# Four graph layers in one pipeline: the transposed features made a stage earlier, and two steps added to the order of the work

## The chip, the cores and the metric

The kernel runs on one core of a Trainium2 chip. The metric is the device time of one launch in microseconds (us); the time of a kernel is the median of several runs. Before the change it is 5589.18 us (three runs, 5588.3 to 5589.55). In what follows PE is the tensor engine (matmuls; its weight loads are a row of their own, PEld), DVE the vector engine, ACT the scalar engine, POOL the general-purpose engine, and SP the engine that issues the DMAs.

## What is computed

Input x holds 64 graphs ("images") of 256 nodes with 128 features, adj their 256 x 256 adjacency matrices of zeros and ones, each row with a few tens of ones. Four layers follow each other, and each ends with a residual and a layernorm:

```python
def _layernorm(x, axis=-1, eps=1e-5):
    m = jnp.mean(x, axis=axis, keepdims=True)
    v = jnp.var(x, axis=axis, keepdims=True)
    return (x - m) / jnp.sqrt(v + eps)
# layer 0: maximum over the neighbours
p = x @ (W1 - W2); q = x @ W2
h = relu(p[:, :, None, :] + q[:, None, :, :] + b) * adj[..., None]
x = _layernorm(x + max(h, axis=2))
# layer 1: in, out and node representations (elu), two aggregations with adj, tanh of a product
# layer 2: two steps of normalised aggregation with elu between
# layer 3: for every pair of nodes a message
pre = m_j[:, None, :, :] + m_i[:, :, None, :] + b1
msg = gelu(layernorm(pre, g1, be1))
agg = einsum('bijo,bij->bio', msg, adj)
x = _layernorm(x + layernorm(concat([x, agg]) @ W2 + b2))
```

Layers 0 and 3 touch every edge: the maximum of layer 0, and in layer 3 a layernorm over the features and a Gelu for every edge. They are most of the work.

## The kernel before

**Edges as slots.** For each image the neighbours of every node are numbered, and the nodes are ordered by how many they have. Slot s of a node is its s-th neighbour, and 40 slots suffice. The slots, cut to the nodes that can have as many, make one line of 4800 columns for each half h of the neighbours (WIDTH, from RECTS, L27). A matrix `hot` of zeros and ones (in an 8-bit format) picks the neighbour of each column, so that one matmul with `hot` as the moving operand gathers features: L668 gathers q for layer 0 (three bf16 parts of q, so three matmuls per 512 columns), L731 gathers c for layer 3. L684 adds corrections for slots that a node lacks.

**Layer 0** (`layer_0`, L643): the features xn are transposed by PE (`to_features`, L201: two transposes L205 and a copy by ACT L207) into xT, multiplied with the weights w0qp (L650), and the neighbours' part is split in three (`split3`, L494: q by ACT, the rest by DVE L498 to L500). For each half and each 512 columns L668 and L684 fill a PSUM tile `bigp`; the first is copied by ACT into `lanes` (L686), DVE folds the others into it by maximum (`fold`, L481, recorded under L492 and L488). After the last one `total_m` (L691) is the maximum of the two lanes; PE transposes it (L694), ACT copies it to `mk` (L695), and L702 puts the nodes back into their own order.

**Layer 3** works on tiles of 1024 columns, 704 at the end: five tiles in each half, ten in all (TODO, L716). `sums_of` (L721) makes one tile of `pre`: L731 gathers, DVE adds the node's own part (L735), ACT squares (L739), PE sums the squares over the features (L746), ACT adds eps (`row`, L748), and a DMA lays the row into DRAM (`line`, L753). After every second tile the two rows are fetched as a small tile `vr` of up to 128 x 16 (L765), with a mask `fu` (L767); ACT takes the square root and DVE the reciprocal (`inverse_root`, L70 to L73), DVE multiplies by the mask (L772), and a DMA writes the scales to DRAM (`scale_line`, L774). In `last` (L828) a scale row is fetched, spread over all partitions (`rs_s`, L835), two tiles ahead of its use; DVE multiplies (L846), ACT takes the Gelu (L848), DVE folds by addition (`sums`, L492), and PE multiplies the fold by the weights (L867) and puts the nodes in order (L877). `sums_of` runs four tiles ahead (AHEAD). `inverse_root` also serves the layernorms (rs, L174) and the degrees (dinv, L270).

**Tables of ACT.** Sqrt, Exp, Tanh and Gelu need different function tables on ACT; wherever one follows another in ACT's order, the compiler puts a table load ahead of it.

**Stages and order.** An image passes four stages: `first` (slots and `hot`, L502), `second` (layers 0 and 1), `third` (layer 2 and the first four tiles of layer 3), `last` (the rest). In one step the four stages work on four successive images, 64 + 3 steps in all, written out without a loop (UNROLL, L40). The stages are Python generators; each `yield` ends a piece. `together` (L339) always takes the next piece of the generator that is least far along, measured as pieces taken over a weight; the weights are the numbers in STAGES (L886), which are the numbers of pieces. So another `yield` or another weight moves all pieces of a step against each other. What comes out is the order in which the pieces are recorded; a scheduler of the language then makes each engine's own list out of it, which need not follow the recorded order exactly. Each engine works its list strictly in order, and so does SP with its DMAs. PSUM is split into four tiles `mm` and four tiles `bigp`; a tile is reused when it has been read.

Of the kernel before, what the change touches and what calls it, by code (L numbers as in the profile page):

```python
# [9 lines left out]
F32 = mybir.dt.float32  # L10
BF16 = mybir.dt.bfloat16
AF = mybir.ActivationFunctionType
# [7 lines left out]
P = 128  # L20
# [23 lines left out]
def kernel(  # L44
# [9 lines left out]
    nc = tc.nc  # L54
# [15 lines left out]
    def inverse_root(t):  # L70

        nc.scalar.activation(t, t, AF.Sqrt)  # L72
        nc.vector.reciprocal(t, t)  # L73

    def load(src, shape, name):
        t = consts.tile(shape, F32, name=name)
        nc.sync.dma_start(t, src)
        return t
# [4 lines left out]
    def spread(src, name):  # L83
        return load(bass.AP(tensor=src.tensor, offset=src.offset, ap=[[0, P], [1, P]]), [P, P], name)

    w0 = load(l0_w.rearrange("(c p) o -> p c o", p=P), [P, 2, P], "w0")
    w0qp = consts.tile([P, 2, P], F32, name="w0qp")
    nc.vector.tensor_copy(w0qp[:, 0], w0[:, 1])
    nc.vector.tensor_sub(w0qp[:, 1], w0[:, 0], w0[:, 1])
    b0 = column(l0_b, "b0")  # L90
    b0s = spread(l0_b, "b0s")

# [27 lines left out]
    with tc.tile_pool(name="prep", bufs=1) as prep, tc.tile_pool(  # L120
        name="ps_prep", bufs=2, space=bass.MemoryType.PSUM
    ) as ps_prep:

        def transposed(dst, src, shape, name, part=lambda t: t):
            t = prep.tile(shape, F32, name=name)
            nc.sync.dma_start(t, src)
            for d, s in part(t) if dst is None else [(dst, t)]:
                pt = ps_prep.tile([P, P], F32, name="pt")
                nc.tensor.transpose(pt, s, ident)
                nc.vector.tensor_copy(d, pt)  # L130

        transposed(w1_ioT[:, :P], l1_w_in, [P, P], "w1_in")
        transposed(w1_ioT[:, P:], l1_w_out, [P, P], "w1_out")
        transposed(w1_nodeT, l1_w_node, [P, P], "w1_node")
        transposed(
            None, l1_w_upd.rearrange("o (c k) -> o c k", k=P), [P, 3, P], "w1_upd",
            lambda t: [(w1_updT[:, c], t[:, c]) for c in range(3)],
        )
        w3 = prep.tile([P, 2, P], F32, name="w3")
        nc.sync.dma_start(w3, l3_w1.rearrange("(c p) o -> p c o", p=P))  # L140
        w3m = prep.tile([P, 2], F32, name="w3m")
        nc.vector.tensor_reduce(w3m, w3, AX.X, ALU.add)
        nc.vector.tensor_scalar(w3m, w3m, 1.0 / P, None, ALU.mult)
        for c in range(2):
            nc.vector.tensor_scalar(w3c[:, c], w3[:, c], w3m[:, c:c + 1], None, ALU.subtract)
        b3 = prep.tile([P, 1], F32, name="b3")
        nc.sync.dma_start(b3, bass.AP(tensor=l3_b1.tensor, offset=l3_b1.offset, ap=[[1, P], [1, 1]]))
        invp = prep.tile([P, P], F32, name="invp")
        nc.vector.memset(invp, 1.0 / P)
        pb = ps_prep.tile([P, P], F32, name="pt")  # L150
        nc.tensor.matmul(pb[:, :1], invp, b3, start=True, stop=True)
        nc.vector.tensor_sub(b3c, b3, pb[:, :1])


    class Shared:
# [5 lines left out]
        def psum(self):  # L161
            return self.ps_mm.tile([P, 512], F32, name="mm")
# [173 lines left out]
    def by_half(pt):  # L336
        return pt[:, :N].rearrange("p (h d) -> p h d", h=H)
# [14 lines left out]
    def sparse(ctx):  # L352
# [102 lines left out]
        sh = Shared(work, state, ps_mm)  # L455
# [46 lines left out]
        def first(g, s):  # L502

            xn = state.tile([P, H, P], F32, name="x0", bufs=3)
# [25 lines left out]
            for hi in range(H):  # L530
                for h in range(H):
                    c = (hi * H + h) * 2
# [38 lines left out]
            permT = hold.tile([P, H, H, N], F32, name="permT")  # L571
# [17 lines left out]
            lack = hold.tile([ROWS, H, N], BF16, name="lack")  # L589
# [5 lines left out]
            for h in range(H):  # L595
                for hk in range(H):
                    c = (h * H + hk) * 2
# [10 lines left out]
            lack_t = state.tile([ROWS, H, g_n, g_w], BF16, name="lack_t")  # L608
# [15 lines left out]
            hot = hold.tile([P, H, WIDTH], FP8, name="hot")  # L624
# [8 lines left out]
            for h in range(H):  # L633
# [5 lines left out]
                    saturate=False,  # L639
                )  # L640
            s["hot"] = hot

        def layer_0(s):  # L643

            xn, hot, lack, lack_t, permT = (s[n] for n in ("xn", "hot", "lack", "lack_t", "permT"))
            xT = sh.to_features(xn, "xT_0", 1)
            yield
            pq = psum()
            for h in range(H):
                nc.tensor.matmul(  # L650
                    pq[:, h * N:(h + 1) * N], xT[:, h * P:(h + 1) * P], w0qp.rearrange("p c o -> p (c o)"),
                    start=True, stop=True,
                )
            pq = pq.rearrange("p (h c o) -> p h c o", h=H, c=2)
            q3 = work.tile([P, 3, H, P], BF16, name="q3")
            split3(q3, pq[:, :, 0])
            own = work.tile([P, H, P], F32, name="own")
            for h in range(H):
                nc.vector.tensor_add(own[:, h], pq[:, h, 1], b0s)
            yield  # L660
            mk = work.tile([P, H, H, P], F32, name="mk")
            for h in range(H):
                lanes = work.tile([P, 2, N], F32, name="lanes")
                for t0 in range(0, WIDTH, 512):
                    tl = min(512, WIDTH - t0)
                    pt = ps_big.tile([P, 512], F32, name="bigp")
                    for i in range(3):
                        nc.tensor.matmul(  # L668
                            pt[:, :tl], q3[:, i, h], hot[:, h, t0:t0 + tl], start=i == 0, stop=False
                        )  # L670
                    todo = []
                    for s0, n, w, at in pieces(t0, t0 + tl):
                        if s0 >= g_s0:
                            todo.append((pt[:, at:at + n * w], low, lack_t[:, h].rearrange("p s k -> p (s k)")))
                            continue
                        for i in range(n):
                            m = SURE[s0 + i]
                            if m < w:
                                c = at + i * w
                                todo.append((pt[:, c + m:c + w], pick_of(s0 + i), lack[:, h, m:w]))  # L680
                    if not todo:
                        todo.append((pt[:, :2], pick_of(0), lack[:, h, 0:2]))
                    for i, (o_, l_, r_) in enumerate(todo):
                        nc.tensor.matmul(o_, l_, r_, start=False, stop=i == len(todo) - 1)  # L684
                    if t0 == 0:
                        nc.scalar.copy(lanes, pt.rearrange("p (s k) -> p s k", s=2))  # L686
                    else:
                        fold(lanes, pt, t0, tl, ALU.max)
                    yield
                mx = work.tile([P, N], F32, name="total_m")  # L690
                nc.vector.tensor_max(mx, lanes[:, 0], lanes[:, 1])  # L691
                pt = psum()
                for hk in range(H):
                    nc.tensor.transpose(pt[:, hk * P:(hk + 1) * P], mx[:, hk * P:(hk + 1) * P], ident)  # L694
                nc.scalar.copy(mk[:, h], by_half(pt))  # L695
                yield
            pm = psum()
            for h in range(H):
                for hi in range(H):
                    c = h * N + hi * P  # L700
                    for hk in range(H):
                        nc.tensor.matmul(  # L702
                            pm[:, c:c + P], permT[:, h, hk, hi * P:(hi + 1) * P], mk[:, h, hk],
                            start=hk == 0, stop=hk == H - 1,
                        )
            yield
            m0 = work.tile([P, H, P], F32, name="m0")
            nc.scalar.copy(m0, by_half(pm))
            nc.vector.tensor_max(m0, pm[:, N:].rearrange("p (h d) -> p h d", h=H), m0)
            nc.vector.tensor_add(m0, m0, own)  # L710
            y = work.tile([P, H, P], F32, name="y", bufs=2)
            nc.vector.scalar_tensor_tensor(y, m0, 0.0, xn, ALU.max, ALU.add)
            s["x1"] = sh.node_tile("x1")
            yield from sh.layernorm(s["x1"], y)
# [6 lines left out]
        def sums_of(s, i):  # L721

            h, t0, tl = TODO[i]
            hot, c3, dT = s["hot"], s["c3"], s["dT"]
# [36 lines left out]
            n = at + tl  # L761
            rows = n // PIECE
            first_at = TODO[i - GROUP + 1][0] * WIDTH + TODO[i - GROUP + 1][1]
            vr = big.tile([P, PIECE], F32, name="vr")
# [3 lines left out]
                fu[:rows],  # L768
                s["fulls"].rearrange("h w -> (h w)")[first_at:first_at + n].rearrange("(p k) -> p k", k=PIECE),
            )  # L770
            inverse_root(vr[:rows])
            nc.vector.tensor_mul(vr[:rows], vr[:rows], fu[:rows])  # L772
            out_line = dram.tile([1, GROUP * TILE], F32, name="scale_line")
            nc.sync.dma_start(out_line[:, :n].rearrange("o (p k) -> (o p) k", k=PIECE), vr[:rows])  # L774
# [108 lines left out]


        U = next(u for u in (UNROLL, 8, 4, 2, 1) if B % u == 0)
        STAGES = [(last, 34), (third, 34), (second, 42), (first, 17)]  # L886

        def steps(g0):
            ss = [{} for _ in range(U)]
# [216 lines left out]
    with tc.tile_pool(name="flag", bufs=1) as fp, tc.tile_pool(  # L1106
        name="ps_flag", bufs=1, space=bass.MemoryType.PSUM
# [44 lines left out]
```

## Time and profile before

| | |
|---|---|
| median of three runs | 5589.18 us (5588.3 to 5589.55) |
| profiled execution, its own time | 5585.87 us |
| its span, first to last instruction | 5583.8 us |
| mean granted clock of PE | 0.876 |
| DMA moved | 365.17 MB, 65 GB/s |
| ACT table loads | 447 at L72, 447 at L848, 133 at L192, 63 at L252, 61 at L196, 1283 ns each |
| one step in the steady part | 85.0 us |

The profile is one execution, recorded by the hardware. Its page gives busy time by engine; the view of waits gives who waited for whom, in total; the view of groups gives each kind of instruction with its mean duration; the timeline shows instructions one after the other, with the idle time ahead of them in brackets and what ended it; the view by windows gives busy time and granted clock in stretches of time. "L735" is line 735 of the kernel as printed above. The engines run at the same time, and a wait costs something only if the engine that waits is late for the end.

### The profile page before, as it was taken

To read this page: it belongs to the slowest core of one execution; us is meant where nothing else is said; L and a number is where in the kernel's file an instruction comes from. 1 tells how busy PE (TensorE), PEld (TensorE's weight loads), DVE (VectorE), ACT (ScalarE), POOL (GpSimd) and SP (SyncE) were. 2 spreads that over 40 slices of the span, in tenths; PEclk is the share of its full clock that TensorE was granted. 3 is DMA by queue.
4 is the path that set the end of the run, shared out by engine and by line. 5 is a ranking of instruction groups with operands and counts; after the bars stand their busy time and mean duration, and the time that the engine had idled before them with its cause. 6 is when DMAs were issued, how large, how long until landed. Compare 5 with 4: busy or idle time off the path is not lost.

```text
span 5583.8 us, 83622 instructions
## 1 busy us (share of the span) xinstructions
PE 4511.0 (81%) x27408; PEld 2487.9 (45%) x27408; DVE 4805.5 (86%) x14654; ACT 4218.5 (76%) x6465; POOL 2.0 (0%) x10
## 2 busy tenths in 40 slices
PE   5888888888788888887887888888888878888884
PEld 3444444444444444444444444444444444444442
DVE  7788888898888888888988888889888888888886
ACT  2777777777777777777777777777777777777776
POOL 0000000000000000000000000000000000000000
PEclk8888888888888888888888888888888888888886
DMA  0212222222222122222222222221222222212212
GB/s 24 65 59 72 67 63 66 72 65 66 66 65 70 60 72 67 63 66 74 63 66 67 70 66 61 69 67 63 71 70 63 66 67 70 66 59 71 64 59 76
DMA packets 292814, 365.17 MB, mean 65 GB/s; under 512 B 151952, under 2 KB 210448, under 8 KB 292368
## 3 DMA queue, kind: packets, MB, share of 16 engines
q1 hardware_dynamic: 292368, 359.73, 20.8%
q8 instruction: 218, 3.57, 0.3%
q14 instruction: 228, 1.87, 0.1%
HBM read 345.07 MB, written 14.53 MB: 64 GB/s over the span
## 4 chain that ended last, share of the span: by engine, by line
PE 42%; DVE 34%; ACT 17%; issue 5%; DMA 3%; SPq 0%; DVEq 0%; POOL 0%; ACTq 0%; POOLq 0%
PE bigp L731 8%; PE bigp L668 8%; DVE lanes L492 8%; DVE pre L735 6%; ACT L72 6%; DVE hot L628 5%; DVE sums L492 5%; PE mm L867 4%; DVE pre L846 3%; PE mm L746 3%; PE mm L877 2%; PE mm L817 2%; PE mm L294 2%; DMA rs_s<-scale_line 2%; ACT sums L848 2%
## 5 line engine op out<-in xcount | busy, mean ns | idle before, releaser
L668 PE MATMUL bigp<-hot,q 128*128 128x512 fp8e4 (+1 forms) x3840 | 1117.5, 391 | 206.2 <-DVE lanes L492 179.7
L731 PE MATMUL bigp<-hot,c 128*128 128x512 fp8e4 (+1 forms) x3840 | 1010.6, 395 | 136.0 <-DVE pre L735 77.1
L735 DVE TENSOR_TENSOR pre<-bigp,dT 128x512 f32<-128x512 f32 (+6 forms) x1664 | 841.4, 534 | 252.2 <-PE bigp L731 245.9
L739 ACT ACTIVATE sq<-pre 128x1024 f32<-128x1024 f32 (+1 forms) x640 | 636.6, 995 | 273.2 <-DVE rs L73 196.9
L492 DVE TENSOR_TENSOR lanes<-bigp,lanes 128x512 f32<-128x512 f32 (+6 forms) x1536 | 769.3, 501 | 12.2 <-ACT vr L72 2.9
L846 DVE TENSOR_TENSOR pre<-pre,rs_s 128x1024 f32<-128x1024 f32 (+1 forms) x640 | 734.4, 1148 | 35.6 <-DMA rs_s<-scale_line 34.5
L492 DVE TENSOR_TENSOR sums<-pre,sums 128x1024 f32<-128x1024 f32 (+6 forms) x1024 | 628.3, 614 | 11.6 <-ACT pre L848 11.2
L848 ACT ACTIVATE pre<-pre,be,g 128x1024 f32<-128x1024 f32 (+1 forms) x512 | 600.0, 1172 | 11.0 <-DVE pre L846 6.9
L731 PEld LDWEIGHTS <-c 128*128 128x128 bf16 x3840 | 346.2, 102 | 544.5 <-issue 268.1
L848 ACT ACT_TABLE_LOAD x447 | 573.5, 1283 | 7.9
L72 ACT ACT_TABLE_LOAD x447 | 573.5, 1283 | 7.9
L748 ACT ACTIVATE row<-mm,eps_t 128x256 f32<-128x256 f32 (+1 forms) x640 | 293.5, 459 | 361.9 <-PE mm L746 351.0
L668 PEld LDWEIGHTS <-q 128*128 128x128 bf16 x3840 | 309.6, 100 | 514.9 <-DVE lanes L492 186.5
L746 PE MATMUL mm<-sq,ones 128*32 128x256 f32 (+1 forms) x5120 | 436.5, 418 | 113.7 <-ACT sq L739 110.7
L628 DVE TENSOR_SCALAR hot<-rank 128x512 fp8e4<-128x512 bf16 (+5 forms) x1536 | 485.4, 345 | 0.0
L684 PEld LDWEIGHTS <-pick 42*128 42x128 bf16 x2944 | 154.5, 95 | 449.6 <-issue 435.2
L650 PE MATMUL mm<-w0qp,xT 128*128 128x256 f32 x256 | 130.0, 662 | 266.3 <-ACT xT L207 266.3
L867 PE MATMUL mm<-w3u,sums 128*128 128x128 f32 x2048 | 293.8, 287 | 44.9 <-DVE sums L492 44.9
L867 PEld LDWEIGHTS mm<-w3u,sums 128*128 128x128 f32 x2048 | 258.7, 195 | 75.9 <-PE bigp L731 39.6
L684 PE MATMUL bigp<-lack,pick 42*128 42x36 bf16 (+16 forms) x2944 | 275.8, 187 | 0.0
L746 PEld LDWEIGHTS mm<-sq,ones 128*32 128x32 f32 x5120 | 107.2, 115 | 352.5 <-ACT sq L739 162.0
L73 DVE RECIPROCAL vr<-vr 128x16 f32<-128x16 f32 (+1 forms) x320 | 79.5, 249 | 161.7 <-ACT vr L72 161.6
(227 smaller groups left out, 7319.0 us busy)
## 6 DMA issues: line engine op xcount, KB each, us to landing
rs_s<-scale_line SPq DMA_DIRECT2D x512, 512.0 KB
rs_s<-scale_line SPq DMA_DIRECT2D x128, 352.0 KB
an<-in_adj SPq DMA_DIRECT2D x64, 256.0 KB
x<-in_x SPq DMA_DIRECT2D x64, 128.0 KB
line<-row SPq DMA_DIRECT2D x512, 4.0 KB
out<-o SPq DMA_DIRECT2D x64, 128.0 KB
fu<-fulls SPq DMA_DIRECT2D x192, 4.0 KB
vr<-line SPq DMA_DIRECT2D x192, 8.0 KB
```

The lines of the kernel that those rows point to most:

```text
L72: nc.scalar.activation(t, t, AF.Sqrt)
L492: nc.vector.tensor_tensor(lanes[:, :k, :w], src[:, i:i + k], lanes[:, :k, :w], op)
L628: nc.vector.tensor_scalar(hot[:, :, at:at + w], rank[:, :, :w], s0 + i + 1.0 - FAR, None, ALU.is_equal, saturate=False)
L668: nc.tensor.matmul(pt[:, :tl], q3[:, i, h], hot[:, h, t0:t0 + tl], start=i == 0, stop=False)
L684: nc.tensor.matmul(o_, l_, r_, start=False, stop=i == len(todo) - 1)
L731: nc.tensor.matmul(pt[:, :bl], c3[:, k, h], hot[:, h, t0 + b:t0 + b + bl], start=k == 0, stop=k == 2)
L735: nc.vector.tensor_add(block(pre[:, b:], n, w, at), block(pt, n, w, at), widen(dT[:, h, :w], n))
L739: nc.scalar.activation(sq[:, :tl], pre[:, :tl], AF.Square)
L746: nc.tensor.matmul(pr[q * Q:(q + 1) * Q, :tl // 4], ones[:, :Q], v4[:, :, q], start=True, stop=True)
L846: nc.vector.tensor_mul(pre[:, :tl], pre[:, :tl], rs[:, :tl])
L848: nc.scalar.activation(msg[:, :tl], pre[:, :tl], AF.Gelu, bias=be3, scale=g3)
L867: nc.tensor.matmul(pt[:, cols], lanes[:, k, cols], w3u[:, 1], start=k == 0, stop=False)
```

## The change

Three edits and what goes with them. The transposed features of layer 0 are made at the end of `first` instead of at the start of `layer_0`, with the pool's usual two buffers instead of one; the `yield` behind them goes. A `yield` is put between `total_m` and its transposes. In `sums_of` the call of `inverse_root` is written out, with a `yield` between Sqrt and reciprocal; it lies in each of the five groups of an image, two of them in `third` and three in `last`. The weights of the stages follow the numbers of pieces. The load of w0 and the two DVE instructions that make w0qp of it move into the preparation, so that w0 gives its memory back after it.

```diff
-    w0 = load(l0_w.rearrange("(c p) o -> p c o", p=P), [P, 2, P], "w0")
     w0qp = consts.tile([P, 2, P], F32, name="w0qp")
-    nc.vector.tensor_copy(w0qp[:, 0], w0[:, 1])
-    nc.vector.tensor_sub(w0qp[:, 1], w0[:, 0], w0[:, 1])
...
+        w0 = prep.tile([P, 2, P], F32, name="w0")
+        nc.sync.dma_start(w0, l0_w.rearrange("(c p) o -> p c o", p=P))
+        nc.vector.tensor_copy(w0qp[:, 0], w0[:, 1])
+        nc.vector.tensor_sub(w0qp[:, 1], w0[:, 0], w0[:, 1])
         w3 = prep.tile([P, 2, P], F32, name="w3")
...
             s["hot"] = hot
+            s["xT"] = sh.to_features(xn, "xT_0")
 
         def layer_0(s):
 
-            xn, hot, lack, lack_t, permT = (s[n] for n in ("xn", "hot", "lack", "lack_t", "permT"))
-            xT = sh.to_features(xn, "xT_0", 1)
-            yield
+            xn, xT, hot, lack, lack_t, permT = (s[n] for n in ("xn", "xT", "hot", "lack", "lack_t", "permT"))
             pq = psum()
...
                 nc.vector.tensor_max(mx, lanes[:, 0], lanes[:, 1])
+                yield
                 pt = psum()
...
-            inverse_root(vr[:rows])
+            nc.scalar.activation(vr[:rows], vr[:rows], AF.Sqrt)
+            yield
+            nc.vector.reciprocal(vr[:rows], vr[:rows])
             nc.vector.tensor_mul(vr[:rows], vr[:rows], fu[:rows])
...
-        STAGES = [(last, 34), (third, 34), (second, 42), (first, 17)]
+        STAGES = [(last, 37), (third, 36), (second, 43), (first, 17)]
```

## What was predicted

> **What bounds the kernel now.** I read the page first: busy time by engine.
>
> ```profile
> PE 4511.0 (81%) x27408; PEld 2487.9 (45%) x27408; DVE 4805.5 (86%) x14654; ACT 4218.5 (76%) x6465; POOL 2.0 (0%) x10
> ```
>
> VectorE (DVE) is the fullest engine: 4805.5 us of 5583.8. The other 778 us are what a change of order can win on it, 12.2 us for each of the 64 images. So the second view is the table of waits, for DVE and for what DVE waits behind:
>
> ```profile
> DVE pre L735 <- PE bigp L731: 245.9, 308, 2.4
> ...
> DVE vr L73 <- ACT vr L72: 161.6, 127, 2.2
> ...
> PE mm L650 <- ACT xT L207: 266.3, 64, 4.5
> ...
> DVE io L224 <- PE mm L221: 70.7, 61, 3.1
> ...
> DVE y L328 <- PE mm L877: 62.0, 64, 4.8
> ...
> DVE pre L846 <- DMA rs_s<-scale_line: 34.5, 51, 5.6
> ```
>
> (Columns: total us, times, longest.) 127 waits of the reciprocal are two of the five per image; L650 waits once per image, 4.2 us each time. Third, one steady step in the timeline (output DMAs at 2725.67 and 2810.68: a step takes 85.0 us). ScalarE (ACT) where two steps meet:
>
> ```profile
> 2720.24 1.28 ACT L252 ACT_TABLE_LOAD   x1
> 2721.53 0.42 ACT L252 ACTIVATE y<-y 128x256 f32<-128x256 f32 x1
> 2721.97 1.28 ACT L72 ACT_TABLE_LOAD   x1
> 2723.26 0.32 ACT L72 ACTIVATE rs<-rs 128x2 f32<-128x2 f32 x2
> 2723.49 0.77 ACT L739 ACTIVATE sq<-pre 128x704 f32<-128x704 f32 x1
> 2724.17 0.35 ACT L207 COPY xT<-mm 128x256 f32<-128x256 f32 x1
> ```
>
> Here PE has transposed the features by 2720.05 and then stands still until xT is copied; on DVE the same stretch reads:
>
> ```profile
> 2729.18 0.25 DVE L73 RECIPROCAL vr<-vr 128x16 f32<-128x16 f32 x1 [1.89 <-ACT vr L72]
> ...
> 2731.92 0.69 DVE L735 TENSOR_TENSOR pre<-bigp,dT 128x512 f32<-128x512 f32 x1 [1.01 <-PE bigp L731]
> ...
> 2734.55 0.69 DVE L735 TENSOR_TENSOR pre<-bigp,dT 128x512 f32<-128x512 f32 x1 [1.80 <-PE bigp L731]
> ```
>
> Between 2715.57 (L328) and 2735.24 DVE idles 0.89+0.15+0.18+1.89+1.01+1.80 = 5.9 us, more than half of the some 10 us that its timeline marks in a step. The last view is the table by windows; the third figure from the end of a row is the granted clock:
>
> ```profile
> 2723.00:2733.00 10.00, 8.16 (x30) 3.24 (x30) 6.44 (x21) 9.43 (x16) 0.00 (x0) 0.50 0.29 96
> 2733.00:2767.00 34.00, 30.08 (x203) 13.99 (x202) 31.05 (x86) 25.73 (x43) 0.00 (x0) 1.00 0.21 63
> ```
>
> After the 4.3 us in front of L650, PE runs at half clock for 10 us. Below I also use the order in which both programs' instructions stand on each engine; it holds no times.
>
> **The change, part by part.** The numbers of instructions on DVE, PE and SP stay the same, but ACT gets 1,213 table loads for 1,152. The order moves everywhere, since the stage weights changed with the added steps (34/34/42 to 37/36/43), and it now repeats every two steps: I call the two kinds of meeting X and Y.
>
> *Features transposed a stage ahead.* From the tanh (end 2721.95) to xT (2724.17) ACT now does a table load, two square roots and a Square, 2.2 us. In the new order xT stands directly behind the tanh in X and Y: 2.2 us earlier. L650 then takes 2.08 us (2724.57 to 2726.65), but the copy q of its result starts at 2729.05, 2.4 us late, behind two aT copies (0.65), a load (1.28), a Gelu (1.24), a load (1.28) and the Sqrt of vr (0.22). In X only a Square (0.77) stands between, less than L650's 2.08: all 2.4 are won. In Y it is Square, load and Gelu, 0.77+1.28+1.24 = 3.29, so q is late by 1.2 and 1.2 are won. So q comes 4.6 or 3.4 us earlier, 4.0 on average. Not all arrives at DVE: today PE does L731 for DVE after two L668; then it does three L668 first, and before the second L731 six L668 with their corrections (X), or the four matmuls of L527/L528 (Y). At the half-clock pitch of 0.43 us (L731 x3 in 1.28) I count some 1.5 us for that. Net **-2.5 us per step**. Bounds: 0 (DVE finds another wait of the same length) to -5.9 (all idle time of the stretch).
>
> *Step between Sqrt and reciprocal.* Three of the five reciprocals per image wait for nothing now. That of the middle waits 0.83 us (at 2744.58), with dense DVE work behind it until 2756; in the new order several DVE instructions stand between, so **-0.8 us**. The 1.89 at 2729.18 is no second gain: behind it stands rest (L498), which needs q from 2729.40 on; it goes only together with the 2.5 above. What is late next: behind the reciprocal stand the product with fu and, on SP, the DMA of scale_line, then fu and two rs_s, in order. The tile that reads them is multiplied at L846, which waits 34.5 us in all today. The first group of an image now has its reciprocal ahead of y (L328) instead of behind z, so it isn't later there. I take 0, bounds -0.5 and +0.5 us per step (34.5/64 gone, or the same again).
>
> *Step behind the last maximum.* PE waits 109.1 us for total_m at L694, DVE waits for nothing behind it; PE idles there while DVE is busy (2764 to 2768). Other matmuls move ahead of the transposes. 0; bounds 0 and -109.1/64 = -1.7 us (if all of it were on the path).
>
> *Table loads.* 61 more at 1.28 us are 78 us of ACT, which idles 1,365 us; ACT holds 17% of the chain that ended last, so I take 0.17 x 78 = 13 us, **+0.2 per step**; bounds 0 and 78 us. A rule speaks against this edit: the Trainium skill, "ScalarE: Activation LUTs", section "What ACT_TABLE_LOAD costs", adds a drain of about 1.38 us to the 1.28 of a load. In this trace the Gelu behind the load at 2725.08 starts at 2726.38, 20 ns after it, and the work ahead of the load ends 20 ns before it: no drain shows. By the rule the 61 loads would take an estimated 162 us of ACT, and the term would be 28 us.
>
> *New order before y.* In the new order all of L236 and L238 stand ahead of the eight products L877 that y (L328) needs; today half of L236 and all of L238 (0.44+0.88 us) follow them. DVE has less work left before y, and I let y wait 0.4 us longer of these 1.3: **+0.4 per step**; bounds 0 and 1.3.
>
> *Moved weight load.* w0 goes from first to 23rd on SP; an issue is 0.45 us, so 22 loads start that much earlier and w0 some 10 us later. It is read first at 47.8 us (L650). 0, bounds -0.5 and +0.5 us once. xT_0 has two buffers, w0 gives its place back after the preparation: nothing in the time.
>
> Sum: -2.5 - 0.8 + 0.2 + 0.4 = -2.7 us per step, times some 62 full steps (64 images, the first and last stretches thin) = -167 us. The profiled execution took 5585.87 us, 2.1 around its span, and lies 3.3 below the median of 5589.18; the sum goes on the median: 5589 - 167 = **5422 us**.
>
> **The rivals.**
>
> *PE stays at full clock where the steps meet.* With xT 2.2 us earlier, PE idles 2.1 instead of 4.3 us before L650. The rows at half clock: L650 2.08 us, three L731 in 1.28, against 0.66 (2733.69) at full clock. Then the waits of 1.01 and 1.80 at L735 go as well, say 2.5 more: -5.2 x 62 = 5267 us. Against it: at 2788 the clock is 0.50 after two gaps of only 0.80 and 1.07 us around 0.59 us of work. The Trainium skill, "TensorE: Matmul & The Clock Gate", section "What's actually happening", asks for an idle window of about 3.4 us; by it this rival would be the forecast, at 5267, but the row at 2788 disagrees.
>
> *The clock drops elsewhere.* This is the one that ends slower. In Y the aggregate products L867 no longer stand ahead of the 24 L731 but behind the transposes of x1 (L205), which need x from DVE. From the DVE rows between the fourth pre and x (0.3+1.1+0.4+1.1+0.1+1.2+0.3 = 4.5, less one group of L731, 0.66) PE idles 3.8 us there. At half clock the eight L867 with their small ones take 5.1 instead of 2.5 us, and io (L224) waits 2.6 us longer; what follows (L323, L877, L236, L238, 4 to 5 us of work at full clock) adds some 2. In every step that is 4.6 - 2.7 = +1.9, times 62 = +118: 5707 us; it decides once PE idles there some 3 us in X as well (1.2+0.8+0.3 less 0.66 = 1.7 by the same rows). In Y alone it is 2.3 - 2.7 = -0.4 per step, 5564 us.
>
> *The gain is swapped for equal waits*, above all at kc (L541), which in Y stands behind L205 and L527/L528 on PE: up to 3 us every second step, and no clock gained. 5589 us. That the change doesn't do what it says is excluded for the order, which shows xT and the reciprocals moved.
>
> **How the numbers follow.** Forecast, 5360 to 5500: 0.50. Full clock, 5230 to 5340: 0.15. Half-lost gain, 5500 to 5578: 0.12. Equal, within 0.2% (11 us, about what a measurement of this kernel can tell from no change): 0.05. Slower, to 5720: 0.18. Faster 0.50+0.15+0.12 = 0.77. The range leaves out half of the full-clock case (0.08) and two thirds of the slower one (0.12): 5265 to 5640.
>
> **What would show it.** Right: the wait of vr's reciprocal under 40 us; L650 waiting for xT about 130 instead of 266 us; DVE busy the same 4805 in a span 2 to 4% shorter; ACT's table loads 1,213 at 1.28. Full clock: the granted clock above 0.92 and L735's wait for L731 under 100 us. Slower: the granted clock below 0.86 and io's wait for L221 above 200 us. I am wrong if DVE's waits move to kc, L735 or elu in the same size.

## The result, and the profile after

The changed kernel takes **5603.3 us** (median; 5589.88 to 5619.32), against 5588.99 for the kernel before in the same series: a ratio of 1.0024, with a 95% interval from 1.0016 to 1.0032. It is slower by a quarter of a per cent, where 3% less was predicted. The prediction's wide range, 5265 to 5640, takes the time in, but only by its slow side, which was there for rivals; the forecast of 5422 and its direction are wrong. Its profiled execution took 5599.96 us, with a span of 5597.9 and a mean granted clock of 0.896 (before: 5585.87, 5583.8, 0.876).

Busy time by engine, and the shares of the chain that ended last (followed back from the last instruction, at each step to what released it), from the page of the changed kernel; the last line is the chain of the kernel before:

```profile
PE 4533.3 (81%) x27408; PEld 2551.9 (46%) x27408; DVE 4810.7 (86%) x14654; ACT 4291.8 (77%) x6526; POOL 1.8 (0%) x10
...
PE 39%; DVE 29%; ACT 18%; DMA 7%; issue 7%; SPq 0%; ACTq 0%; DVEq 0%
...
PE 42%; DVE 34%; ACT 17%; issue 5%; DMA 3%; SPq 0%; DVEq 0%; POOL 0%; ACTq 0%; POOLq 0%
```

DVE is as busy as before (4805.5), and it idles as long: 5597.9 - 4810.7 = 787 us for 778. ACT has its 61 table loads more (6526 instructions for 6465) and 73 us more work. In the chain DMA has 7% for 3%, and DVE and PE have less (29% for 34%, 39% for 42%). So nothing was won on the fullest engine; its waits are where the change must be read. The view of waits of the changed kernel (total us, times, longest; line numbers are up to three higher than before):

```profile
DVE io L225 <- PE mm L222: 162.0, 64, 3.9
DVE pre L849 <- DMA rs_s<-scale_line: 79.9, 107, 1.9
DVE elu_e L199 <- ACT elu_e L193: 61.4, 122, 1.3
DVE pre L736 <- PE bigp L732: 54.2, 63, 1.3
DVE y L329 <- PE mm L880: 49.8, 64, 5.3
DVE kc L542 <- PE mm L534: 49.3, 32, 2.2
DVE aT L276 <- PE mm L237: 47.8, 59, 2.6
DVE vr L774 <- ACT vr L772: 36.0, 63, 1.1
DVE dinv L73 <- ACT dinv L72: 33.5, 31, 2.0
...
PE mm L650 <- ACT xT L208: 144.1, 64, 2.9
...
PE mm L870 <- DVE sums L493: 119.5, 63, 14.6
...
PE mm L206 <- DVE x L179: 244.7, 199, 4.1
```

What the change aims at has come true: pre's wait for the gathers fell from 245.9 to 54.2, that of vr's reciprocal from 161.6 to 36.0, and L650 waits 144.1 for xT instead of 266.3. On DVE that is 192 + 126 = 318 us of idle time (pre and vr), 5.1 us per step. All of it, and 9 us more, stands in other rows: io +91, elu_e +60, aT +47, kc +48, rs_s +45, dinv +29, and small ones. And PE waits 119.5 us instead of 44.9 for the fold (L870, L867 before), and 244.7 instead of 58.1 for the normalised features that it transposes (L206, L205 before).

The place where two steps meet looks as predicted. ACT, from the timeline of the changed kernel (a meeting of kind X):

```profile
2735.86 0.42 ACT L253 ACTIVATE y<-y 128x256 f32<-128x256 f32 x1
2736.18 0.35 ACT L208 COPY xT<-mm 128x256 f32<-128x256 f32 x1
2736.44 0.79 ACT L740 ACTIVATE sq<-pre 128x704 f32<-128x704 f32 x1
2738.18 0.37 ACT L498 CAST q<-mm 128x256 bf16<-128x256 f32 x1 [0.95 <-PE mm L650]
```

xT follows the tanh at once, and q follows L650 at once; the loads, the Gelu and the square roots that stood between come later. DVE's two waits for the gathers here are 1.17 and 0.93 us (1.01 and 1.80 before), and the 1.89 of the reciprocal is gone. L650 itself, at half clock in 61 of 64 images before (2.0 us or more), takes 1.2 us or less in 19 images now, and 2.0 or more in 16.

So the gain is there; where in the step is it lost? The table gives the time of some marks, counted from the start of L650, as a mean over the 42 steps that start between 1000 and 4600 us in each of the two traces.

| mark | before, us | changed, us |
|---|---|---|
| ACT copies q (L497, now L498) | 4.50 | 2.54 |
| DVE makes the last `total_m` (L691) | 46.06 | 45.94 |
| DVE makes x1, the x that ends layer 0 (L178, now L179) | 61.32 | 63.06 |
| DVE makes io (L224, now L225) | 67.15 | 69.70 |
| PE starts the aggregate products of the second half (L867, now L870) | 70.71 | 73.25 |
| PE ends L247 (now L248) | 79.79 | 82.30 |
| next L650 | 85.25 | 85.55 |

The meeting is won twice: xT comes 2.2 us earlier behind L248 (85.55 - 82.30 = 3.25 us for 5.46), and q another 2.0 us earlier behind L650. At the last `total_m` the 2.0 us are gone. At x1 the step is 1.7 us late, and at io 2.5. From there to L248 both kernels take the same time. So what the meeting wins is lost in the middle of the step, between q and io.

What PE does around io, first before:

```profile
2786.15 0.59 PE L205 MATMUL mm<-ident,x 128*128 128x128 f32 x2 [0.80 <-DVE x L178]
...
2789.82 1.77 PE L221 MATMUL mm<-w_ioT,xT 128*128 128x256 f32 x4
...
2795.20 1.13 PE L867 MATMUL mm<-w3u,sums 128*128 128x128 f32 x8 [0.46 <-DVE sums L492]
```

and in the changed kernel:

```profile
2885.61 0.33 PE L206 MATMUL mm<-ident,x 128*128 128x128 f32 x1 [2.00 <-DVE x L179]
...
2886.11 0.83 PE L870 MATMUL mm<-w3u,sums 128*128 128x128 f32 x6
...
2887.08 1.87 PE L870 MATMUL mm<-w3u,sums 128*128 128x128 f32 x8
...
2889.21 1.88 PE L222 MATMUL mm<-w_ioT,xT 128*128 128x256 f32 x4
```

PE now stands still for 2.9 us in a mean step, instead of 0.9, until x1 is there; the aggregate products of the first half, done earlier before, follow only then, and from these transposes to io's matmuls (L222) it takes 4.6 us instead of 3.6. In the step shown they run at half clock: eight products take 1.87 us, and 1.13 at full clock. DVE waits 2.22 us for io there (1.11 before, in the step at 2706).

The end of the step is not where the loss lies. From the first of the second half's products to the end of L248 it takes 8.7 or 8.8 us in 53 of 62 steps, less than the 9.08 of before; in 9 steps it takes 10.2 to 11.8. One of the slow ones starts at 2808.10, with the granted clock (third from the end in the view by windows) at half for most of it:

```profile
2810.00:2816.00 6.00, 6.00 (x26) 4.26 (x27) 2.68 (x14) 3.23 (x5) 0.00 (x0) 0.53 0.03 5
```

### The profile page after: what moved, and what is told of

It is laid out like the page before. It is cut to its first block, busy times and chain, and to the rows that moved or that the text cites. A ratio compares the mean times of both kernels' runs of the same rounds, so it can differ in the third digit from the quotient of the medians.

```text
span 5597.9 us, 84027 instructions
## 1 busy us (share of the span) xinstructions
PE 4533.3 (81%) x27408; PEld 2551.9 (46%) x27408; DVE 4810.7 (86%) x14654; ACT 4291.8 (77%) x6526; POOL 1.8 (0%) x10
## 3 DMA queue, kind: packets, MB, share of 16 engines
q14 instruction: 230, 1.88, 0.1%
## 4 chain that ended last, share of the span: by engine, by line
PE 39%; DVE 29%; ACT 18%; DMA 7%; issue 7%; SPq 0%; ACTq 0%; DVEq 0%
DVE lanes L493 7%; PE bigp L668 6%; PE mm L870 6%; PE bigp L732 5%; DMA rs_s<-scale_line 5%; DVE pre L736 5%; DVE sums L493 4%; DVE pre L849 3%; PE mm L747 3%; ACT sq L740 3%; ACT L193 2%; PE mm L295 2%; PE mm L222 2%; ACT L851 2%; DVE hot L629 2%
## 5 line engine op out<-in xcount | busy, mean ns | idle before, releaser
L668 PE MATMUL bigp<-hot,q 128*128 128x512 fp8e4 (+1 forms) x3840 | 1097.0, 382 | 71.9 <-ACT q L498 42.9
L732 PE MATMUL bigp<-hot,c 128*128 128x512 fp8e4 (+1 forms) x3840 | 952.3, 375 | 79.0 <-DVE pre L736 66.9
L736 DVE TENSOR_TENSOR pre<-bigp,dT 128x512 f32<-128x512 f32 (+6 forms) x1664 | 860.5, 536 | 56.8 <-PE bigp L732 54.2
L849 DVE TENSOR_TENSOR pre<-pre,rs_s 128x1024 f32<-128x1024 f32 (+1 forms) x640 | 737.3, 1153 | 80.8 <-DMA rs_s<-scale_line 79.9
L747 PE MATMUL mm<-sq,ones 128*32 128x256 f32 (+1 forms) x5120 | 462.0, 420 | 289.6 <-ACT sq L740 285.0
L870 PE MATMUL mm<-w3u,sums 128*128 128x128 f32 x2048 | 381.2, 339 | 119.5 <-DVE sums L493 119.5
L870 PEld LDWEIGHTS mm<-w3u,sums 128*128 128x128 f32 x2048 | 332.7, 242 | 152.0 <-issue 105.4
L206 PE MATMUL mm<-ident,x 128*128 128x128 f32 x512 | 154.6, 324 | 244.9 <-DVE x L179 244.7
```

The source lines that it names most:

```text
L668: nc.tensor.matmul(pt[:, :tl], q3[:, i, h], hot[:, h, t0:t0 + tl], start=i == 0, stop=False)
L732: nc.tensor.matmul(pt[:, :bl], c3[:, k, h], hot[:, h, t0 + b:t0 + b + bl], start=k == 0, stop=k == 2)
L736: nc.vector.tensor_add(block(pre[:, b:], n, w, at), block(pt, n, w, at), widen(dT[:, h, :w], n))
L747: nc.tensor.matmul(pr[q * Q:(q + 1) * Q, :tl // 4], ones[:, :Q], v4[:, :, q], start=True, stop=True)
L849: nc.vector.tensor_mul(pre[:, :tl], pre[:, :tl], rs[:, :tl])
L870: nc.tensor.matmul(pt[:, cols], lanes[:, k, cols], w3u[:, 1], start=k == 0, stop=False)
```

## The experiments

The line numbers of each kernel differ by a few from those of before. Two steps hold 454 instructions on DVE and 1058 on PE. Of them, some 260 and 720 still stand in the sequence of before in the changed kernel's trace (the longest common sequence).

| kernel | edits and weights (last/third/second) | median us | ratio to before, 95% | loads | DVE idle us |
|---|---|---|---|---|---|
| before | 34/34/42 | 5589 | 1 | 1152 | 778 |
| the change | all, 37/36/43 | 5603 | 1.0024 [1.0016, 1.0032] | 1213 | 787 |
| a_only | xT, 34/34/41 | 5652 | 1.0111 [1.0094, 1.0128] | 1336 | 851 |
| b_only | reciprocal, 37/36/42 | 5793 | 1.0362 [1.0344, 1.0379] | 1094 | 1012 |
| c_only | maximum, 34/34/44 | 5560 | 0.9951 [0.9935, 0.9968] | 1145 | 755 |
| ab_only | 37/36/41 | 5888 | 1.0537 [1.0520, 1.0555] | 1210 | 1078 |
| ac_only | 34/34/43 | 5798 | 1.0379 [1.0361, 1.0396] | 1213 | 950 |
| bc_only | 37/36/44 | 5927 | 1.0615 [1.0598, 1.0633] | 1214 | 1058 |
| weights_only | none, 37/36/42 | 5470 | 0.9779 [0.9763, 0.9795] | 1274 | 673 |
| a_still | xT, 34/34/42 | 5620 | 1.0057 [1.0041, 1.0074] | 1154 | 834 |
| b_still | reciprocal, 34/34/42 | 5587 | 1.0000 [0.9990, 1.0010] | 1152 | 774 |
| c_still | maximum, 34/34/42 | 5523 | 0.9884 [0.9868, 0.9901] | 1150 | 723 |
| abc_still | all, 34/34/42 | 5483 | 0.9809 [0.9783, 0.9835] | 1093 | 681 |
| abc_weight44 | all, 37/36/44 | 5832 | 1.0425 [1.0404, 1.0446] | 1203 | 1019 |
| b_after_io | reciprocal + a yield | 5415 | 0.9687 [0.9671, 0.9703] | 1096 | 630 |
| abc_after_io | the change + a yield | 5913 | 1.0581 [1.0563, 1.0599] | 1180 | 1071 |
| b_filled | reciprocal + 8 gathers | 5789 | 1.0360 [1.0343, 1.0378] | 1093 | 993 |
| b_after_io_c | b_after_io + maximum | 5798 | 1.0380 [1.0362, 1.0397] | 1086 | 990 |
| abc_after_io_late | abc_after_io, diff later | 5980 | 1.0703 [1.0686, 1.0719] | 1180 | 1144 |
| b_after_io_late | b_after_io, diff later | 5757 | 1.0300 [1.0286, 1.0314] | 1163 | 958 |

(DVE idle is span less DVE's busy time, which lies between 4785 and 4851 us in all of them.)

**The three edits one by one.** Each kernel is the one before with one edit or two of the diff shown above, and the weights that follow the pieces. Three theories stood against each other: S, the sum of the prediction's terms; L, the table loads set the time; W, a new order only swaps one wait for another.

> The features transposed in the stage first, nothing else of the change (weights 34/34/41). Theory S (each edit is worth the wait that it takes away, as the prediction summed them): q comes earlier where the steps meet, -2.5 us per step, against 184 more table loads at 1.28 us on ACT, of which 17% on the path: about 5475 us. Theory L (ACT's table loads set the time): 1,336 loads for 1,152 are up to +236 us, 5700 to 5825. Theory W (an order only swaps one wait of DVE for another): 5560 to 5620, L650's wait for xT near half of before, DVE's idle time within 40 us of 780, with new waits of DVE at other lines of the same sum.

> Only the step between Sqrt and reciprocal, with weights 37/36/42. S: the middle reciprocal's 0.83 us per step is won and the one where the steps meet gives way to q: about 5535 us. L: 1,094 loads for 1,152, -74 us: about 5515. W: 5560 to 5620; the reciprocal's wait of 161.6 us falls under 60, and the wait for the scales' DMA or for PE grows by as much.

> Only the step behind the last maximum, with weights 34/34/44. S: DVE waits for nothing there, 5589 us. L: 1,145 loads for 1,152, 5580. W: 5560 to 5620, PE's wait for total_m at L694 smaller than 109 us and no gain from it.

> Features and the step at the reciprocal, without the step behind the maximum (37/36/41). S: both gains, about 5420 us. L: 1,210 loads as in the changed kernel (1,213): 5600. W: 5560 to 5620, as the changed kernel.

Measured: 5652, 5793, 5560 and 5888. S falls: the two edits that should win lose, the one priced at nothing wins. L falls: a_only has the most table loads of the four and loses least of the three that lose; b_only has 58 fewer than before and takes 204 us more. W is right that DVE only waits elsewhere, but its range holds for c_only alone. Where b_only's time lies shows in its waits:

```profile
DVE aT L275 <- PE mm L236: 215.9, 62, 3.6
DVE y L328 <- PE mm L879: 180.5, 64, 6.3
...
PE mm L869 <- DVE hot L628: 214.0, 59, 3.8
```

The aggregate products of the second half (L869 here) stand ahead of L746, L236 and L238 on PE's list in b_only, and behind the last gathers; PE stands before them for 3.6 us in every step until DVE's fold is done, and then works at half clock (2.05 us for eight products, in the mean of all steps). The view names `hot` L628, the DVE instruction that ended last before them; in b_filled below it names the fold at the same place. All that waits for L236 and L879 waits with them. This gave a new theory, T: the edit loses because PE stands in front of these products, and what is behind them on the list is late.

**The products put behind those with aT.** One more yield, for the second half only:

```diff
                 yield
+                if h == 1:
+                    yield
 
                 pt = psum()
```

> The edit at the reciprocal alone (weights 37/36/42), and one more yield ahead of the aggregate products of the second half, so that on PE they stand behind L746 and the four products with aT and an (L236, L238) instead of ahead of them. Theory T (what costs in the edit at the reciprocal is that these products stand on PE's list waiting for DVE's fold, and all behind them waits too, at half clock): DVE's wait for aT goes from 216 us to under 80, PE's wait of the products stays but blocks less, time from 5793 to 5620-5700. Rival U (the place of these products is incidental, the loss is spread over the whole order): 5760-5830.

> The whole change, and the same extra yield ahead of the aggregate products of the second half only. Theory T: the 119 us that PE waits for the fold no longer lie ahead of L237 and L239, DVE's wait for aT goes from 48 to under 20 us: 5540-5590, faster than the change. Rival U: an order like another, 5590-5650.

b_after_io takes 5415 us: 378 less than b_only, more than T asked for, and the fastest kernel of all, 3.1% below before. Two lines of its waits answer to those of b_only; the wait for aT has no line of its own among the largest any more, and PE's wait for the fold is 18.0 us:

```profile
DVE y L328 <- PE mm L881: 62.6, 64, 3.5
...
PE mm L871 <- DVE sums L492: 18.0, 3, 14.5
```

But the same yield in the whole change gives 5913 us, 310 more than without it, where T said 5540 to 5590. DVE's wait for aT did fall as T said (47.8 to 21), and the time rose all the same: T explains b_only and doesn't carry over.

**PE kept at work during the wait.** b_only with eight gathers more, ahead of the same products:

```diff
                 pt = psum()
+                if h == 1:
+                    for i in range(8):
+                        nc.tensor.matmul(pt, s["c3"][:, 0, h], s["hot"][:, h, :512], start=True, stop=True)
```

> The edit at the reciprocal alone (weights 37/36/42), and eight extra gathers of 512 columns into the tile that the aggregate products of the second half overwrite, issued right ahead of them: PE works for 1.7 us (3.5 at half clock) of the some 3.6 in which it waits for the fold. They add 8 x 64 matmuls that change no output. If the half clock behind the wait is what costs (T, clock): the sixteen products take 1.0 instead of 2.05 per eight, L746 and L236 half as well, 1.5 to 2.9 us per step back, 5610-5700, and the granted clock rises above 0.86 from 0.845. If the wait itself costs and the clock does not (T, wait): 5780-5800. If the eight gathers are late themselves (rival): 5800-5900.

Measured 5789, the 5793 of b_only within its scatter. The timeline of b_filled shows that the gathers (L868) did not go where they were meant to go:

```profile
2799.71 1.89 PE L868 MATMUL mm<-hot,c 128*128 128x512 fp8e4 x8
...
2802.40 0.41 PE L731 MATMUL bigp<-hot,c 128*128 128x192 fp8e4 x3 [0.16 <-DVE pre L735]
2806.52 2.07 PE L872 MATMUL mm<-w3u,sums 128*128 128x128 f32 x8 [3.71 <-DVE sums L492]
```

They stand ahead of the L731 in PE's list and filled another wait, of 1.88 us in b_only; the 3.71 us ahead of the products and their half clock remain. So the run is no test of what the half clock costs. It shows only that a wait of 1.88 us per step on PE went (the mean granted clock rose from 0.845 to 0.865) and the time did not.

**The weights alone.** The kernel before with `STAGES = [(last, 37), (third, 36), (second, 42), (first, 17)]` and nothing else.

> The kernel before with the weights 37/36/42 of the edit at the reciprocal, and no added yield: no instruction added or taken away, the same pieces in another order. If the weights alone set the order that loses (V): 5700-5850. If the cut between Sqrt and reciprocal does (X): 5570-5620, within 0.6% of before. By the prediction's way of counting (every edit is priced by what it issues): 5589.

Measured 5470, 2.2% faster than before, with the same instructions and 122 table loads more. Neither V nor X foresaw it. The order that the weights make is worth two thirds of all that the prediction added up; some 800 of the 1058 PE instructions of two steps, but only some 240 of 454 on DVE, stand in the sequence of before. It even does what the first edit was made for: L650's wait for xT falls from 266.3 to 15.2 us, and L650 takes 1.13 us, not 2.08, in nearly every image.

**The edits without new pieces or weights.** In each, the `yield` that follows the added one is taken out, or the one behind the transposed features is kept though it ends an empty piece, and the weights of before stay; for the reciprocal:

```diff
-            inverse_root(vr[:rows])
+            nc.scalar.activation(vr[:rows], vr[:rows], AF.Sqrt)
+            yield
+            nc.vector.reciprocal(vr[:rows], vr[:rows])
...
                 at += TODO[j][2]
-            yield
```

> All three edits, but each keeps the number of pieces: where an edit adds a yield, the yield behind it goes (so the reciprocal, its product and its DMA fall into the piece that follows), and where the features move, the empty yield stays. The weights stay 34/34/42/17. On PE the order from perm_f (L817) to the next L650 is the one of before, instruction for instruction; 1,093 table loads. Theory N (the prediction's terms are right where the order at the end of the step doesn't move; the loss of the change came from the new weights and pieces): -2.5 for xT and -0.8 for the reciprocal per step, 62 steps: 5385, within 5340 to 5480. Theory O (any new order swaps one wait of DVE for another, also where the end stays as it was): 5500-5700.

> The edit at the reciprocal alone, with as many pieces as before (the yield behind the group goes) and the weights of before; 1,152 table loads. On PE the order at the end of the step is that of before. N: -0.8 us per step, 5540, within 5510 to 5575. O: anywhere from 5450 to 5700, with no less waiting of DVE in all than the 778 us of before.

> The yield behind the last maximum alone, with the yield behind its transposes taken out and the weights of before: only the matmuls around the transposes of total_m trade places. N: 0, 5575 to 5600. O: 5450 to 5700.

> The features' transposes alone moved a stage ahead, the empty yield kept, the weights of before; 1,154 table loads. The scheduler nevertheless moves the end of the step: the transposes of x1 come 14 gathers earlier on PE, and L877 stands whole ahead of the products with aT and an. N: the price of the place where steps meet, -2.5 us per step, 5434, within 5400 to 5500, if the moved end costs nothing. O: the moved end takes it back, 5560-5700, as in the edit with its weight (5652).

b_still gives exactly before: in the two steps that I compared, every engine has the same instructions in the same sequence, so moving a yield by a few instructions moved nothing. c_still wins 1.2%, where N said nothing would change. a_still loses 0.6%; of its end O was right: DVE's waits at the gathers fall to 121.7 us, but new ones come, of 131.4 (dinv) and 107.6 (hs), and PE's wait for the fold is 109.5. Together the three win 1.9%: 106 us, half of the 205 that N asked for, and outside N's range by 3 us. The trace shows the end of the step (PE from L817 to L650) in the order of before in 31 of 62 steps, every second one; the expectation said in all. Here, waits went and did not come back in the same size:

```profile
DVE pre L736 <- PE bigp L732: 170.2, 191, 3.4
...
DVE vr L774 <- ACT vr L772: 18.9, 37, 1.8
...
PE mm L651 <- ACT xT L208: 211.8, 63, 3.7
```

pre's wait is 76 us less than before, vr's 143 less, io's 48 less; of that, m (57.7), kc (48.2) and lanes (27.8) took back 127.

**The rest of the table, and one weight by one.**

> The change without its edit at the reciprocal (weights 34/34/43). If the edits' prices added up from the single ones (+63 for the features, -29 for the maximum, with 5589): 5623. The prediction's terms: -2.5 per step, 5434. Theory T (the end of the step decides: here the aggregate products of both halves keep their places of before, L868's wait stays under 60 us): the gain where steps meet remains in part, 5480-5620.

> The change without the move of the features (weights 37/36/44). If single prices added up (+204 and -29): 5764. The prediction's terms: -0.8 per step, 5540. T: on PE the products of the second half stand behind only two gathers, but four of the products with permT follow ahead of those with aT, so the wait for the fold is passed on to y rather than to aT: 5600-5760.

> The whole change with one number altered: the weight of second 44 instead of 43. The same instructions. The aggregate products of the second half now stand directly ahead of the products with aT and an (L237, L239) in both kinds of step, as with the first two edits without the third (5888). T: PE's wait for the fold is over 200 us in all and passes on to DVE's wait for aT, 5750-5900. If the time hangs on what the edits issue and not on where the scheduler puts it: 5603, within 15.

> The fastest so far (the edit at the reciprocal, weights 37/36/42, one yield more ahead of the second half's aggregate products, 5415), with the yield behind the last maximum moved ahead of its transposes as in the kernel that gave -1.2% alone. If gains add: 5415 - 66 = 5350. If an order is a new draw each time: 5400-5700.

Measured 5798, 5927, 5832 and 5798. The single prices do not add: +63, +204 and -29 us would put the whole change at 5827, and it is 5603; a pair costs more than its parts in all three cases. Of T's three ranges only that for abc_weight44 held; ac_only and bc_only lie far above theirs. One weight changed by one, with the same instructions, moves the change by 228 us. In abc_weight44 the aggregate products stand directly ahead of those with aT, and the waits are those that T names:

```profile
DVE aT L276 <- PE mm L237: 130.6, 94, 3.4
DVE diff L512 <- DMA an<-in_adj: 127.6, 48, 4.3
...
PE mm L870 <- DVE sums L493: 252.9, 64, 14.7
```

b_after_io_c asked whether two gains add (5415 and -66): they give 5798.

**One wait taken away, the order kept.** In abc_after_io, diff of the next image (L512) stands on DVE right behind the load of its adjacency, and DVE waits for that load. The edit ties diff to a later value (the ACT instruction that reads diff moves with it):

```diff
-            nc.vector.scalar_tensor_tensor(diff, an, -1.0, an, ALU.add, ALU.mult)
...
             nc.vector.scalar_tensor_tensor(kc, pc, -1.0, down_c, ALU.mult, ALU.subtract)
+            neg = work.tile([P, 1], F32, name="neg")
+            nc.vector.tensor_scalar(neg, kc[:, 0, 0:1], 0.0, -1.0, ALU.mult, ALU.add)
+            nc.vector.scalar_tensor_tensor(diff, an, neg, an, ALU.add, ALU.mult)
```

> The whole change with the extra yield (5913), and diff (L512) tied to a later value: its factor -1 is made by one small DVE instruction from kc, so diff can't stand right behind the load of the next image's adjacency any more, where DVE waited 196 us in all for that load. PE and SP keep their order, instruction for instruction, and of 454 DVE instructions in two steps 451 keep their place. If a wait that is taken away comes back at the end (V): -196 and +10 for the 64 small instructions, 5727, within 5690 to 5780. If DVE then waits as long elsewhere (U): 5880-5930.

> The fastest so far (5415), with the factor of diff made by one small DVE instruction from nz, which puts diff behind nz of its own image: DVE waited 131 us in all for the load there. This moves the rest somewhat: of two steps some 80 of 454 DVE and 85 of 1058 PE instructions change places. V: -131 and +10, 5294, within 5260 to 5350, if the moved instructions cost nothing. U: 5400-5600.

abc_after_io_late takes 5980 us: not 186 less, but 67 more. The wait for the load was 195.8 us in all in abc_after_io and is gone; in its place two others grew, that of y from 71.1 and that of pre for rs_s from 96.7:

```profile
DVE diff L512 <- DMA an<-in_adj: 195.8, 59, 4.7
...
DVE pre L849 <- DMA rs_s<-scale_line: 96.7, 81, 6.0
...
DVE y L329 <- PE mm L882: 71.1, 35, 5.5
```

and with diff later:

```profile
DVE pre L851 <- DMA rs_s<-scale_line: 232.4, 75, 7.5
DVE y L329 <- PE mm L884: 175.2, 34, 6.4
```

For y, the reason is seen in one step of abc_after_io itself. Its DVE waits 3.08 us for the load up to 2783.80. At that time the chain that ended last isn't on DVE at all; it goes along PE without a gap:

```profile
2779.29 1.71 PE mm L239 x4
2780.99 1.61 PE mm L872 x8
...
2784.54 0.89 PE mm L882 x8
...
2786.55 1.34 PE mm L248 x12
```

DVE needed L882 for y next. It waited for the load while PE was on its way there, and after diff it still waited 2.09 us for L882; without the load it waits for PE all the longer. PE and SP keep their order in the trace, as expected, and on ACT only the two instructions on diff change places. Why rs_s comes later as well I haven't settled; the chain of abc_after_io_late passes there along x's load on SP and a DMA of 4.18 us to rs_s. b_after_io_late, in which 80 DVE instructions change places, takes 5757 instead of 5415; its waits for y (164.0) and rs_s (98.9) grew too. U was right in that nothing was won, but even U expected no loss of that size.

## Why the prediction was wrong

**What came true.** The edits do what the prediction says they do at their own place: vr's wait 36.0 (under 40 was asked), L650's wait 144.1 (about 130), DVE's busy time the same, 1,213 table loads. The 3.3 us per step that it wanted there are 5.1 in the waits, and by the marks above q comes 2.2 + 2.0 = 4.2 us earlier in the step, where it said 4.0.

**The step that failed** is the sum: "Net -2.5 us per step" at the meeting and "-0.8" at the reciprocal were added as if idle time taken from DVE at one place were time taken from the end. DVE is the fullest engine, but at 86% it is not what sets the time from moment to moment: the chain of before passes DVE for 34% only. A wait of DVE is what other chains leave it. abc_after_io_late shows that for one wait, with PE and SP in unchanged order. The prediction took 1.5 us off q's gain for the gathers right behind it and let the rest pass through the whole step. It did not: the last `total_m` comes no earlier than before, and io comes 2.5 us later. The bound "0 (DVE finds another wait of the same length)" was there; it was taken for the far end of a range, and was the likely value. The rival of equal waits, put at 5%, is what happened in kind, but not where it said: kc got 48 and elu_e 60 us, a third of what came back, and io 91. In time the change lies 14 us above before, just outside the 11 us that this rival allowed, in the row of the slower cases.

**Terms that were mis-sized.** The prediction put the middle of the step at nothing, but for the scales: the wait for rs_s, "0, bounds -0.5 and +0.5 us per step", went from 34.5 to 79.9 us, +0.7 per step, and the chain that ended last passes the DMA to rs_s for 5.3% of the span instead of 2.4%. The delay from q to x1, +3.7 us per step by the marks, and that from there to io, +0.8, have no term in the sum; only the rival on the clock names the second. "New order before y", +0.4, was not needed: y's wait fell from 62.0 to 49.8 us, and the end of the step takes as long as before.

**The middle reciprocal**, -0.8: not shown by itself. b_still, meant for it, turned out to be the order of before.

**The maximum**, 0 with bounds 0 and -1.7 us per step: c_still gives -65 us, some -1.0 per step over 62; the bound held and the value was wrong.

**Table loads**, +0.2: no sign of them. weights_only has 1,274 and takes 5470 us, bc_only 1,214 and takes 5927, b_only 1,094 and takes 5793.

**The rival on the clock** ("The clock drops elsewhere") named the right place: the aggregate products behind the transposes of x1, PE idle in front of them, half clock, and io late. PE idles 2.98 us there in the step at 2800 (Y) and 2.00 in the one at 2885 (X), where it said 3.8 and 1.7. The half clock comes only in part of the steps, so it put the size too high: io's wait grew by 91 us, 1.4 per step instead of 2.6, and what follows io added nothing. Its marks were not met: the granted clock of the whole went up (0.876 to 0.896), and io stayed under 200. The rival of full clock came true in part at the meeting (L650 above, and L735's wait for the gathers under 100 us); its clock of 0.92 was not reached, and what it won was lost with the rest.

What stays open: which of the waits between q and io is the cause and which only follows (rs_s, x1, kc and the half clock all grew there, and no run changed one alone), as b_filled didn't hit its mark; and why abc_after_io loses 310 us to one yield, beyond the fact that its waits for the adjacency, for kc and for lanes all grew. The runs settle that the order decides: the same instructions, but for table loads and a few more on DVE or PE, take 5415 to 5980 us by weights, yields and the place of diff, DVE's busy time is the same within 1.4%, and the change's +0.24% is one order among these. What the edits are worth by themselves is not shown: all three with the pieces and weights of before give -1.9%, but the maximum's alone gives -1.2%, the reciprocal's nothing and the features' +0.6%, and new weights with no edit give -2.2%. No single edit has a price of its own.

## What to carry to other kernels

A reordering is not priced at the place that it is meant for: note when a few marks of the step come, before and after, and find the mark at which the gain is lost. Take the mean over many steps, since a single one can be the exception, like the step at 2808 above. For a forecast, follow the chain that ended last through one whole step in the new order, engine by engine, and take a wait on the fullest engine as gain only where that engine carries the chain. Where an edit adds a piece to a scheduled kernel, first keep the number of pieces and the weights, so that more of the rest stays where it is; then try the weights as a separate change (here -2.2% with no edit at all, and b_after_io with -3.1% is the version to keep). And give "the gain turns into equal waits" a large chance when the instructions are the same.

## What was not expected of the hardware

The same wait of PE halved the granted clock in one step and not in the next. In the changed kernel the clock is 0.53 from 2810 to 2816 after a wait of 2.15 us that ended at 2808.10; after a wait of the same 2.15 us at 2639.20 it stays at 1.00. After a wait of 2.22 us L650 takes anything from 1.13 to 1.70 us. The Trainium skill, "TensorE: Matmul & The Clock Gate", section "What's actually happening", speaks of an idle window of about 3.4 us that runs freely. The traces agree with the window: in both kernels all changes of the clock from 300 to 5300 us lie on a grid of 3.41 us. They don't ask for a whole idle window, though. In the kernel before, each of the 175 falls between 300 and 5300 us follows a stretch of the grid in which PE was busy for at most 0.49 of the time, and none of the 940 stretches with PE busy for 0.53 or more at full clock was followed by a fall; in the changed kernel the border lies between 0.47 and 0.60. So, by these figures, a wait of some 2 us that lies within one stretch of the grid (PE busy for 0.4 of it or less) halves the clock behind it, for one to three stretches in most cases, and a wait that is split between two need not.
